# A graph network on one core: the column of dst on ScalarE's queue, and rows of the count matrix at one phase in SBUF

## The chip, the core and the metric

The kernel runs on one core of one Trainium2 chip. The metric is the device time of one execution in microseconds; the time given is the median of several runs. The core has five engines that run side by side, each with its own queue of instructions in program order: TensorE (PE in the profile; its weight loads are listed apart as PEld), VectorE (DVE), ScalarE (ACT), GpSimd (POOL) and SyncE (SP), which here issues DMAs. ScalarE and GpSimd issue some DMAs too. Each partition of SBUF, the memory on the chip, is addressed in bytes, and a tile takes the same byte range in all 128 partitions.

## The reference

A layer norm and a ReLU over 2500 nodes of 256 features, three graph convolutions with the mean over 80000 edges (sorted by dst), a last linear layer over all four states, and the input added at the end:

```python
h = jnp.maximum(_layernorm(x, axis=-1), 0.0)
def _edge_conv(x, src, dst, W, b):
    xi = x[dst]
    xj = x[src]
    m = jnp.concatenate([xi, xj - xi], axis=-1) @ W + b
    s = jax.ops.segment_sum(m, dst, num_segments=N)
    cnt = jax.ops.segment_sum(jnp.ones((dst.shape[0],), m.dtype), dst, num_segments=N)
    return s / jnp.maximum(cnt, 1.0)[:, None]
...
xs = [h]
for W, b in ((W0, b0), (W1, b1), (W2, b2)):
    h = jax.nn.relu(_edge_conv(h, src, dst, W, b))
    xs.append(h)
return x + jnp.concatenate(xs, axis=-1) @ Wf + bf
```

## The kernel before

The kernel never gathers rows of features. It builds the matrix A whose entry (s, d) is the number of edges from node s to node d, and multiplies with it. The nodes d are cut into 417 windows of 6, and the windows into five groups: four of 84 windows (504 columns) and one of 81 (486 columns). The nodes s are cut into 20 tiles of 128. A group's part of A is one SBUF tile `a` of 128 partitions by 20 rows by G = 504 f32 columns (`new_a`, L733), and there are two such buffers, one in each of two pools, used in turn. With 504 columns a row is 2016 bytes long, and the next row follows at once.

**Start (before about 66 us).** The inputs are loaded in a fixed order: `dst` whole on ScalarE's queue (L396), then x in four chunks on SP and ScalarE (L400 to L410). `next_i` (L407 and L408) is a column of dst: for 127 partitions one number each, 4 bytes, 2500 bytes apart in memory, so that each partition knows the first edge of the next partition. From it VectorE makes `after`, `behind` and `pick` (`find_first`, `find_rows`); TensorE multiplies `pick` with `dst` (`pick_half`) and so finds where each window's edges begin; GpSimd then fetches the edges by an indirect DMA. Beside this, VectorE takes the statistics of x (`st`), ScalarE or GpSimd normalizes (`N`), TensorE turns the tiles round (`T`) and multiplies by the weights (`Z` with wb, `F` with wf). All of this stands in one order written out by hand as a string of short names (L849 to L858), which `perform` plays; objects ending in `o` (`SPo`, `ACTo`, `DVEo`) keep program order on their queue, while plain `SP`, `PE`, `DVE` leave it to a scheduler. Before the first pick TensorE runs 22 matmuls on zeros (`warm22`).

**Layer 0 (about 66 to 214 us).** For each group, VectorE compares edge keys with counters (`compare`, tiles one_m and one_n), TensorE multiplies the two 0/1 tiles (`counts`), and ScalarE copies the counts into `a` (`take_counts`). When a group's `a` is ready it is stored to DRAM (`finish`, L788), to be loaded again in layers 1 and 2 (`load_a`, L794). While a group is being built, TensorE multiplies with the group before it (`layer`).

**Layers 1 and 2 (about 214 to 498 us).** For each layer, `nodes_split` (L692) multiplies the states by wb and splits the product into two parts, zh and zl, as float32r; then for each group `layer` (L802) runs, for each of the 20 rows of `a`, four matmuls with that row as the moving operand (L817), then eight in plain f32 with the weights wt (L821), and `final` (L715) adds the last linear layer's share. The order of the groups is such that the two that are still in SBUF come first.

**Small constants.** `brow` holds the three biases, in one partition only (the one of the padding node, `PAD`); `ident` is an identity matrix for turning tiles. Both lie in the pool `const`, which lives through the whole kernel. The pool `pre` (`pp`) lives only through the start, and its space is given to the second buffer of A later.

Of the kernel before, what the change touches and what calls it, by code (L numbers as in the profile page):

```python
# [8 lines left out]
F32 = mybir.dt.float32  # L9
I32 = mybir.dt.int32  # L10
AF = mybir.ActivationFunctionType
OP = mybir.AluOpType
# [4 lines left out]
def general(ctx: ExitStack, tc: tile.TileContext, x, src, dst, Ws, bs, Wf, bf, out):  # L17
# [12 lines left out]
    EB = J * P  # L30
    G = 512
    NG = NP // G
    TG = G // P
    KL = 5
    CELLS = NP * NP
    BIG = 4096.0
    assert E == NCH * P and NCH == NB * J and NP % G == 0 and NT % KL == 0 and EB < BIG
    assert CELLS + EB < 2 ** 24
# [84 lines left out]
    def count_block(b):  # L123
        row = ps_big.tile([P, 2, G], F32, name="big").rearrange("p a n -> p (a n)")
        for j in range(J):
            c = b * J + j
            nc.tensor.transpose(row[:, j * P:(j + 1) * P], key[:, c:c + 1].to_broadcast([P, P]), ident)
        found = bwork.tile([P, J], F32, name="found")
        for j in range(J):
            c = b * J + j  # L130
            junk = bwork.tile([P, EB], F32, name="junk", bufs=1)
            nc.vector.scalar_tensor_tensor(junk, row[:, :EB], key[:, c:c + 1], weight[:, j, :],
                                           op0=OP.is_equal, op1=OP.mult, accum_out=found[:, j:j + 1])
        cell = bwork.tile([P, J], F32, name="cell")
        nc.vector.scalar_tensor_tensor(cell, found, BIG, past[:, b, :], op0=OP.is_lt, op1=OP.mult)
        cell_i = bwork.tile([P, J], I32, name="cell_i")
        nc.vector.tensor_add(cell_i, cell, spare)
        adds = []
        for j in range(J):
            d = nc.gpsimd.indirect_dma_start(  # L140
                out=at[:, :], out_offset=bass.IndirectOffsetOnAxis(ap=cell_i[:, j:j + 1], axis=0),
                in_=found[:, j:j + 1], in_offset=None, compute_op=OP.add)
            for o in adds:
                tc.declare_no_dep(d.ins, o.ins, reason="distinct cells within a block")
            behind(d)
            adds.append(d)
        latest[:] = adds
# [51 lines left out]
    def group(l, g):  # L199
        hl, hn = h[l % 2], h[(l + 1) % 2]  # L200
        pa = ps_big.tile([P, 2, G], F32, name="big")
        if l == 0:
# [39 lines left out]
    for l in range(L):  # L242
        for g in range(NG):
            group(l, g)
# [21 lines left out]
F32R = mybir.dt.float32r  # L266
# [20 lines left out]
def run(it):  # L287
    for _ in it:
        pass
# [16 lines left out]
def chain(*its):  # L306
    for it in its:
        yield from it
# [3 lines left out]
def by_windows(ctx: ExitStack, tc: tile.TileContext, x, src, dst, Ws, bs, Wf, bf, out, missing):  # L312
    nc = tc.nc
    PE, DVE, ACT, POOL, SP = nc.tensor, nc.vector, nc.scalar, nc.gpsimd, nc.sync
    PEo, DVEo, POOLo, ACTo, SPo = (InOrder(tc, e) for e in (PE, DVE, POOL, ACT, SP))
    P = 128
    N, D = x.shape
    E = src.shape[0]
    NT = (N + P - 1) // P
    NP = NT * P  # L320
    LAST = N - (NT - 1) * P
    L = len(Ws)
# [13 lines left out]
    while sum(GWS) < NW:  # L336
        GWS.append(min(84, NW - sum(GWS)))
    G = max(GWS) * W
    NG = len(GWS)
    Q = NT // 2  # L340
    assert NT == 2 * Q
    PAD = 96
# [7 lines left out]
    const = ctx.enter_context(tc.tile_pool(name="const", bufs=1))  # L350
# [9 lines left out]
    def bank():  # L360
        return ps[-1].tile([P, 512], F32, name="bank")
# [8 lines left out]
    away = const.tile([P, WG, CAP], BF16, name="away")  # L370
    cnt = const.tile([P, NP], BF16, name="cnt")
    share = const.tile([P, NT], F32, name="share")
    brow = const.tile([P, L, D], F32, name="brow")
    bf_sb = const.tile([P, D], F32, name="bf_sb")
    ident = const.tile([P, P], F32, name="ident")
    ones = const.tile([P, 1], F32, name="ones")
    ones_b = const.tile([1, 1], BF16, name="ones_b")
    ident_b = const.tile([P, P], BF16, name="ident_b")
# [4 lines left out]
    nc_ = const.tile([P, W + 2], F32, name="nc_")  # L383
    deg_b = const.tile([P, WG, W], BF16, name="deg_b")
    lim = const.tile([P, WG], F32, name="lim")
    a_dram = [dram.tile([P, NT, G], F32, name=f"a_dram{g}") for g in range(NG)]

    apools = [ctx.enter_context(tc.tile_pool(name="apool0", bufs=1))]
    pre = ctx.enter_context(ExitStack())
    pp = pre.enter_context(tc.tile_pool(name="pre", bufs=1))  # L390
    pw = pre.enter_context(tc.tile_pool(name="prework", bufs=2))


    dst_rows = dst.rearrange("(p c) -> p c", p=P)
# [5 lines left out]
    def load_x(queue, a, b):  # L400
        queue.dma_start(acc[:, a:min(b, NT - 1), :], xr[:, a:min(b, NT - 1), :])
        if b == NT:
            queue.dma_start(acc[:LAST, NT - 1, :], x[(NT - 1) * P:N, :])

    chunks = [(0, 2), (2, 6), (6, 12), (12, NT)]
    load_x(SPo, *chunks[0])
    next_i = pp.tile([P, 1], I32, name="next_i")  # L407
    SPo.dma_start(next_i[:P - 1], dst_rows[1:P, 0:1])  # L408
    load_x(SPo, *chunks[1])
    load_x(ACTo, *chunks[2])  # L410
    ws = [None] * L
# [2 lines left out]
    def load_wb(l, queue=SP):  # L414
        ws[l] = wpool.tile([P, DC, D], F32, name="wt"), wpool.tile([P, DC, D], F32, name="wb", bufs=1)
        queue.dma_start(ws[l][1], Ws[l][D:2 * D, :].rearrange("(c p) d -> p c d", p=P))

    def load_wt(l, queue=SP):
        queue.dma_start(ws[l][0], Ws[l][0:D, :].rearrange("(c p) d -> p c d", p=P))
# [19 lines left out]
    POOL.memset(brow, 0.0)  # L439
    nc_i = pp.tile([P, W + 2], I32, name="nc_i")  # L440
    POOL.iota(nc_i, pattern=[[-1, W + 2]], base=1, channel_multiplier=0)
    for l in range(L):
        SP.dma_start(brow[PAD:PAD + 1, l, :], bs[l].rearrange("(o d) -> o d", o=1))
    DVE.memset(ones, 1.0)
    DVE.memset(ones_b, 1.0)
    DVE.memset(cnt[:, NV:], 0.0)
# [199 lines left out]
    turned, pz = {}, {}  # L646
# [45 lines left out]
    def nodes_split(l, t):  # L692
        pz = bank()
        for c in range(DC):
            PE.matmul(pz[:, :D], hT[:, c, t * P:(t + 1) * P], ws[l][1][:, c, :],  # L695
                      start=(c == 0), stop=(c == DC - 1))
        sc = share[:, t:t + 1]
        if t == NT - 1:
            zf = hot.tile([P, D], F32, name="zf")
            DVE.scalar_tensor_tensor(zf, pz[:, :D], sc, brow[:, l, :], op0=OP.mult, op1=OP.add)  # L700
            ACT.copy(zh[:, t, :], zf)
            DVE.tensor_sub(zl[:, t, :], zf, zh[:, t, :].bitcast(F32))
        else:
            ACT.activation(zh[:, t, :], pz[:, :D], AF.Copy, scale=sc)  # L704
            DVE.scalar_tensor_tensor(zl[:, t, :], pz[:, :D], sc, zh[:, t, :].bitcast(F32),  # L705
                                     op0=OP.mult, op1=OP.subtract)

    def add_x(t):
        n = P if t < NT - 1 else LAST
        xb = hot.tile([P, D], F32, name="zf")  # L710
        POOL.dma_start(xb[:n], x[t * P:t * P + n, :])
        POOL.tensor_add(xb[:n], xb[:n], bf_sb[:n])
        POOL.tensor_add(acc[:n, t, :], acc[:n, t, :], xb[:n])
# [15 lines left out]
    def touched(g):  # L729
        c0, n = group_of(g)  # L730
        return [t for t in range(NT) if (t + 1) * P > c0 and t * P < c0 + n]

    def new_a(g):  # L733
        return apools[g % 2].tile([P, NT, G], F32R, name="a")

    windows = [(g, s, min(BW, GWS[g] - s)) for g in range(NG) for s in range(0, GWS[g], BW)]
    ones_of = {}
# [47 lines left out]
    def finish(g, a):  # L785
        c0, n = group_of(g)
        POOLo.tensor_copy(a[PAD:PAD + 1, NT - 1, :n], cnt[PAD:PAD + 1, c0:c0 + n])
        SP.dma_start(a_dram[g][:, :, :n], a[:, :, :n].bitcast(F32))  # L788
        yield
# [43 lines left out]
    a = new_a(0)  # L833
# [39 lines left out]
    def later_loads():  # L873
        load_wb(1, SPo)
        load_wt(1, SPo)
        load_wf(1, SPo)
        SPo.dma_start(bf_sb, bass.AP(tensor=bf.tensor, offset=bf.offset, ap=[[0, P], [1, D]]))
        yield
# [5 lines left out]
    extra = chain(degrees(0), finish(0, a), later_loads(), degrees(1))  # L884
    for g in range(NG):
        at = {}
        own = LATE
        if g + 1 < NG:
            a1 = new_a(g + 1)
# [20 lines left out]
        if g + 1 < NG:  # L910
            run(finish(g + 1, a1))
            held, a = a, a1
# [3 lines left out]
    for l in range(1, L):  # L916
        groups = list(range(NG))
        if l % 2:
            groups.reverse()

        last = touched(groups[0])
        for t in [t for t in range(NT) if t not in last] + last:
            nodes_split(l, t)
        if l + 1 < L:
            load_wb(l + 1)
            load_wt(l + 1)
        finished = set()
        for j, g in enumerate(groups):
            for t in touched(g):
                if t not in finished:  # L930
                    finished.add(t)
                    final(l, t)
                    if l == 1:
                        add_x(t)
            if j == NG - 1:
                load_wf(l + 1)
            run(layer(l, g, tiles[g], LATE))
            if j == 1 and l + 1 < L:
                DVEo.tensor_sub(ws[l + 1][0], ws[l + 1][0], ws[l + 1][1])
            if j + 2 < NG:  # L940
                del tiles[g]
                tiles[groups[j + 2]] = load_a(groups[j + 2])
# [41 lines left out]
```

## Time and profile before

| What | Value |
|---|---|
| median of 3 runs | 521.25 us (520.58 to 522.91) |
| the profiled execution | 522.35 us |
| its span in the profile | 520.4 us |
| mean granted clock of TensorE | 0.997 |
| matmuls on A in layers 1 and 2 (L817) | 800 |
| matmuls on A in layer 0 (line of a helper, L280) | 400 |
| store of one 504-column group of A, issue to landing | 15.4 us (5040 KB) |
| load of one | 15.8 us |
| the same for the 486-column group | 17.1 us and 15.7 us (4860 KB) |

The profile is one execution, told in several views. The page's first part gives each engine's busy time. The chain of waits follows the work that ended last back from the end: what stands in it sets the time, what does not is covered. A group row names the line, the engine, the operation, the tiles as out<-in, the shape and the count, then the busy time and the mean of one, then the engine's idle time just before. Most instructions of the start have the line of a helper, L280, so that they are told apart by their tiles. Matmuls overlap in the pipeline, so their real pace is the distance from start to start.

### The profile page before, as it was taken

Reading aid. Unit: us, or ns where it says so; the run is one execution under the profiler, and the core shown is the slowest. Engines: PE = TensorE matmul, PEld = TensorE weight load, DVE = VectorE, ACT = ScalarE, POOL = GpSimd, SP = SyncE. Lnnn points to the kernel's source line nnn. Section 1 sums busy time; section 2 is a strip of 40 time slices with the busy share of each in tenths; the row PEclk is TensorE's granted clock in tenths of the full one; section 3 lists DMA queues with packets and bytes.
Section 4 is the critical chain, followed back from the end, with each engine's and each line's share of the span. In section 5 each row is a group of like instructions: output and inputs, shape, how many; then the busy total and the mean of one; then the engine's idle time right before and its main releaser. Section 6 shows DMA issues by size and latency. Waiting matters only on the chain.

```text
span 520.4 us, 6987 instructions
## 1 busy us (share of the span) xinstructions
PE 512.0 (98%) x2864; PEld 406.8 (78%) x2864; DVE 213.8 (41%) x455; ACT 138.2 (27%) x307; POOL 69.8 (13%) x102
## 2 busy tenths in 40 slices
PE   7999999999999999999999999999999999999996
PEld 3888878677777778788787878787887878787875
DVE  6899989888797950251101010102501010101033
ACT  5787567553633330340000000003400000000000
POOL 2591000000000000008133323200000000000000
PEclk9999999999999999999999999999999999999999
DMA  9110008840905319001556464100006363630023
GB/s 277 38 51 1 1 2 342 323 203 1 398 1 246 153 34 359 23 20 52 201 232 244 204 247 192 31 1 1 1 0 243 155 248 150 238 145 20 1 82 122
DMA packets 16351, 68.74 MB, mean 132 GB/s; under 512 B 1328, under 2 KB 14152, under 8 KB 15158
## 3 DMA queue, kind: packets, MB, share of 16 engines
q1 hardware_dynamic: 14038, 63.49, 31.2%
q0 software_dynamic: 1344, 3.61, 2.3%
q10 hardware_dynamic: 928, 1.11, 0.7%
q8 instruction: 24, 0.39, 0.3%
q14 instruction: 17, 0.14, 0.1%
HBM read 40.03 MB, written 28.18 MB: 131 GB/s over the span
## 4 chain that ended last, share of the span: by engine, by line
PE 96%; DVE 1%; DMA 1%; issue 0%; ACT 0%; SPq 0%
PE pa L817 35%; PE pa L280 21%; PE bank L718 10%; PE bank L280 9%; PE bank L695 7%; PE pa L821 6%; PE pz L280 6%; DMA next_i<-in_dst_dram 1%; PE turned L280 1%; DVE one_m L280 0%; DVE one_n L280 0%; ACT junk L280 0%; DVE pick L280 0%; DVE zl L280 0%; ACT hT L280 0%
## 5 line engine op out<-in xcount | busy, mean ns | idle before, releaser
L817 PE MATMUL pa<-a,zh 128*128 128x504 f32 (+1 forms) x400 | 157.6, 394 | 0.0
L817 PE MATMUL pa<-a,zl 128*128 128x504 f32 (+1 forms) x400 | 155.5, 389 | 0.0
L720 DVE SCALAR_TENSOR_TENSOR acc<-bank,share,acc 128x256 f32<-128x256 f32 x60 | 29.0, 484 | 214.8 <-PE bank L718 214.8
L817 PEld LDWEIGHTS pa<-a,zh 128*128 128x128 f32 x400 | 75.3, 188 | 15.6
L817 PEld LDWEIGHTS pa<-a,zl 128*128 128x128 f32 x400 | 75.2, 188 | 15.3
L280 PE MATMUL pa<-a,zh 128*128 128x504 f32 (+1 forms) x200 | 85.1, 426 | 0.0
L280 DVE TENSOR_TENSOR one_m<-iota_m,key_m 128x1024 bf16<-128x1024 bf16 (+1 forms) x105 | 71.9, 685 | 15.7 <-PE bank L280 15.4
L280 PE MATMUL pa<-a,zl 128*128 128x504 f32 (+1 forms) x200 | 77.8, 389 | 0.0
L824 ACT ACTIVATE hT<-pa 128x1008 f32<-128x1008 f32 (+1 forms) x10 | 10.0, 1005 | 240.2 <-PE pa L821 240.2
L280 ACT CAST a<-bank 128x480 fp32r<-128x480 f32 (+1 forms) x105 | 54.5, 561 | 66.7 <-PE bank L280 63.9
L280 DVE TENSOR_TENSOR one_n<-iota_n,key_n 128x960 bf16<-128x960 bf16 (+1 forms) x105 | 68.6, 653 | 0.0
L280 PEld LDWEIGHTS <-one_m 128*128 128x128 bf16 x834 | 45.6, 98 | 14.2 <-DVE one_m L280 7.5
L280 PE MATMUL bank<-one_n,one_m 128*128 128x120 bf16 x834 | 54.1, 217 | 0.3 <-DVE one_n L280 0.2
L718 PE MATMUL bank<-wf,hT 128*128 128x256 f32 x240 | 53.6, 379 | 0.0
L718 PEld LDWEIGHTS bank<-wf,hT 128*128 128x128 f32 x240 | 45.6, 190 | 9.9 <-issue 4.1
L280 PEld LDWEIGHTS pa<-a,zh 128*128 128x128 f32 x200 | 37.8, 189 | 9.1 <-issue 2.3
L280 PEld LDWEIGHTS pa<-a,zl 128*128 128x128 f32 x200 | 37.7, 189 | 8.2 <-issue 2.3
L705 DVE SCALAR_TENSOR_TENSOR zl<-bank,share,zh 128x256 fp32r<-128x256 f32 x38 | 18.4, 484 | 56.0 <-ACT zh L704 56.0
L821 PE MATMUL pa<-hT,wt 128*128 128x504 f32 (+1 forms) x80 | 35.2, 583 | 0.0
L695 PE MATMUL bank<-wb,hT 128*128 128x256 f32 x160 | 34.9, 379 | 0.0
L695 PEld LDWEIGHTS bank<-wb,hT 128*128 128x128 f32 x160 | 30.4, 190 | 4.9 <-issue 0.9
L821 PEld LDWEIGHTS pa<-hT,wt 128*128 128x128 f32 x80 | 15.2, 189 | 14.5 <-issue 13.8
(110 smaller groups left out, 339.2 us busy)
## 6 DMA issues: line engine op xcount, KB each, us to landing
a<-a_dram SPq DMA_DIRECT2D x5, 5040.0 KB, 15.8
a_dram<-a SPq DMA_DIRECT2D x4, 5040.0 KB, 15.4
a_dram<-a SPq DMA_DIRECT2D x1, 4860.0 KB, 17.1
a<-a_dram SPq DMA_DIRECT2D x1, 4860.0 KB, 15.7
zf<-in_x_dram POOLq DMA_DIRECT2D x19, 128.0 KB, 2.3
out_dram<-acc SPq DMA_DIRECT2D x19, 128.0 KB, 1.7
wf<-in_L_gnn_Wf_dram SPq DMA_DIRECT2D x4, 256.0 KB
acc<-in_x_dram SPq DMA_DIRECT2D x1, 896.0 KB, 8.4
```

The costliest lines, as they stand in the source:

```text
L280: return self.tc.keep_in_program_order(call(*args, **kwargs))
L695: PE.matmul(pz[:, :D], hT[:, c, t * P:(t + 1) * P], ws[l][1][:, c, :], start=(c == 0), stop=(c == DC - 1))
L705: DVE.scalar_tensor_tensor(zl[:, t, :], pz[:, :D], sc, zh[:, t, :].bitcast(F32), op0=OP.mult, op1=OP.subtract)
L718: PE.matmul(po[:, :D], hT[:, c, t * P:(t + 1) * P], wfs[l][:, c, :], start=(c == 0), stop=(c == DC - 1))
L720: DVE.scalar_tensor_tensor(acc[:, t, :], po[:, :D], share[:, t:t + 1], acc[:, t, :], op0=OP.mult, op1=OP.add)
L817: PE.matmul(pa[:, o, :n], z[:, i, o * P:(o + 1) * P], a[:, i, :n], start=(i == 0 and z is zh), stop=(z is zl and last[o] == (kind, i, o)))
L821: PE.matmul(pa[:, o, :n], ws[l][0][:, c, o * P:(o + 1) * P], hT[:, c, c0:c0 + n], start=False, stop=(last[o] == (kind, i, o)))
L824: ACT.activation(hT[:, :, c0:c0 + n], pa[:, :, :n], AF.Relu)
```

## The change

The column `next_i` is issued on ScalarE's queue, right behind `dst`, and ahead of SP's x chunks in the program. The row length of the tile `a` becomes GS = 512 elements (2048 bytes), of which the first 504 or 486 are used. To make room, `brow` keeps two biases instead of three (the third is loaded into the first's place ahead of layer 2), and `ident` goes from `const` to `pre`. A tile of 24 elements named `between` (96 bytes, never used) is put behind the constants; with it everything that is allocated after `const` begins at 64 modulo 128 bytes. In DRAM the rows of A stay 504 elements apart, so that a store or load of A moves one row at a time.

```diff
+    GS = 512
...
-    brow = const.tile([P, L, D], F32, name="brow")
+    brow = const.tile([P, 2, D], F32, name="brow")
...
-    ident = const.tile([P, P], F32, name="ident")
...
+    const.tile([P, 24], F32, name="between")
...
+    ident = pp.tile([P, P], F32, name="ident")
...
     chunks = [(0, 2), (2, 6), (6, 12), (12, NT)]
+    next_i = pp.tile([P, 1], I32, name="next_i")
+    ACTo.dma_start(next_i[:P - 1], dst_rows[1:P, 0:1])
     load_x(SPo, *chunks[0])
-    next_i = pp.tile([P, 1], I32, name="next_i")
-    SPo.dma_start(next_i[:P - 1], dst_rows[1:P, 0:1])
     load_x(SPo, *chunks[1])
     load_x(ACTo, *chunks[2])
...
-    for l in range(L):
-        SP.dma_start(brow[PAD:PAD + 1, l, :], bs[l].rearrange("(o d) -> o d", o=1))
+    def load_b(l, queue=SP):
+        queue.dma_start(brow[PAD:PAD + 1, l % 2, :], bs[l].rearrange("(o d) -> o d", o=1))
+
+    load_b(0)
+    load_b(1)
...
-            DVE.scalar_tensor_tensor(zf, pz[:, :D], sc, brow[:, l, :], op0=OP.mult, op1=OP.add)
+            DVE.scalar_tensor_tensor(zf, pz[:, :D], sc, brow[:, l % 2, :], op0=OP.mult, op1=OP.add)
...
-        return apools[g % 2].tile([P, NT, G], F32R, name="a")
+        return apools[g % 2].tile([P, NT, GS], F32R, name="a")
...
         if l + 1 < L:
+            load_b(l + 1)
             load_wb(l + 1)
             load_wt(l + 1)
```

## The prediction

> **What bounds the kernel now.** I read the busy line of the page first, then the chain that ended last, then the matmul groups with their shapes kept apart, and at last the first 17 us of the chain and the DMA landings.
>
> ```profile
> PE 512.0 (98%) x2864; PEld 406.8 (78%) x2864; DVE 213.8 (41%) x455; ACT 138.2 (27%) x307; POOL 69.8 (13%) x102
> ...
> PE 96%; DVE 1%; DMA 1%; issue 0%; ACT 0%; SPq 0%
> ...
> L817 PE MATMUL pa<-a,zh 128*128 128x504 f32 x320 | 126.5, 395 | 0.0
> L817 PE MATMUL pa<-a,zl 128*128 128x504 f32 x320 | 124.9, 390 | 0.0
> ...
> 285.18 18.28 PE pa L817 x80
> 303.46 3.38 PE pa L821 x8
> ```
>
> TensorE is busy 98% and is 96% of the chain: what counts is time per matmul, and the holes at the start. The "mean ns of one" of the group rows overlaps its neighbours; the chain gives the true pace: 80 matmuls of 504 columns in 18.28 us, 228.5 ns each. [...]
>
> [...] The built program puts the two A buffers at bytes 148320 and 188640, which is 96 and 224 modulo 256; rows are 2016 B apart, so each begins 32 B lower modulo 256 than the one before. Start to start in the trace, the four matmuls of one row (zh, zl, zh, zl) together, in ns, for the eight 504-column stages of layers 1 and 2, the first two rows and the last left out:
>
> ```
> row begins at (mod 256)    0    32    64    96   128   160   192   224
> four matmuls             917   917   902   918   913   920   910   917
> single ones at 192: 226, 229.5, 229, 226      at 64: 224, 224, 229.5, 224      at 160: 228, 234, 232.5, 225
> ```
>
> The same row number differs by 8 ns between the two buffers, and exactly as this table says, so it is the address, not the place in the stage. The mean is 914.
>
> Now the start:
>
> ```profile
> 1.25 6.42 DMA next_i<-in_dst_dram
> ...
> 7.70 0.15 DVE after L280
> ...
> 8.55 0.76 DVE pick L280
> ...
> 9.45 0.39 PE bank L280
> ...
> 11.66 3.62 PE pz L280 x8
> ...
> 7.70 0.15 DVE L280 CAST after<-next_i 127x1 f32<-127x1 int32 x1 [1.62 <-DMA next_i<-in_dst_dram]
> ...
> 8.45:11.86 3.41, 1.98 (x9) 1.32 (x10) 3.14 (x16) 2.79 (x10) 0.00 (x0) 1.00 1.11 336
> 11.86:15.28 3.42, 3.42 (x9) 2.71 (x9) 3.24 (x17) 1.93 (x7) 2.15 (x2) 0.50 0.51 147
> ```
>
> VectorE stands 1.62 us for the column, and TensorE, whose warm-up ends at about 8.0, waits for pick until 9.45. The last two rows are stages: their columns are busy PE, PEld, DVE, ACT, POOL, then the granted clock: after a thinly used 3.4 us the clock is half for the next 3.4, which costs some 1.7 us of TensorE's work.
>
> [...]the semaphore of next_i steps twice, at 1.72 and 7.67, where a 128-row load shows its engines one by one. [...]of the column's 4-byte packets some 84 run from 3.9 to 4.54, and the other 43 come one per 50 ns from 5.08 to 7.43, in turn with the 1 KB packets (47 ns) of ScalarE's x chunk.[...]
>
> **The change part by part.** *Rows of A.* Now 2048 B apart and the buffers at 146880 and 187840, both 192 modulo 256: every row of every stage begins in the phase that took 910 instead of the mean 914. There are 3 layers of 4 groups of 504 columns and 20 rows, 240 rows at 4 ns: 1.0 us less. For the 60 rows of 486 columns the trace has 881 at 192 against a mean of 882: nothing. What no run shows is a row that follows one of its own phase. Bounds from single matmuls: 224 each would be (228.5 - 224) x 1200 = 5.4 us less; 229.5 each 1.2 us more; 234.5, the highest seen (at 160), 7.2 us more. I take 910, the row as measured: the two cheapest of eight phases are the two that are 64 modulo 128.
>
> *Other matmul operands* (wt, wb, wf, one_m, one_n) move from 224 to 64 modulo 256 with the padding. Row L695 runs at 17.27/80 = 216 ns for 256 f32 columns[...]; nothing is taken, either way up to 0.5 us.
>
> *DMAs of A.* The full-width groups become 2560 pieces of 2016 B instead of 128 of 40320 B. The 486-column group already goes so: its store took 17.1 us against 15.4, its load 15.7 against 15.8. A full one would be 17.1 x 504/486 = 17.7. Loads are issued a stage (25 us) before their use at the least: hidden. Of the stores the first is tightest: issued at 80.84, it would land at 98.6, and the first write of group 2 into that buffer is at 99.89 (trace of ScalarE). Cover 1.3 us; beyond it, each us would stop ScalarE's evictions and then TensorE. Cost nothing. Behind it on SP stand the four loads of later_loads, wanted at 214 and later.
>
> *The column.* It goes from SP, between the first two x chunks, to ScalarE behind dst. On its one engine it begins when dst is through, 3.9, as before. It still has 127 pieces on one engine, and now takes turns with SP's chunks instead of ScalarE's chunk; 84 quickly and 43 at 50 ns end at 7.4 again. Bounds: alone it ends at about 5.2, before VectorE asks (6.08), and all 1.62 us go; in turns from the first, 127 x 57 ns from 3.9 ends at 11.1. I take no change in the landing. SP's issue of x rows 2 to 5, 2.43 us long behind the column now, should be short, and its landing (9.44; VectorE waits 0.17 for it) earlier: 0.2 us less. In exchange ScalarE's x chunk, its table load and the dst cast (4.28) stand behind the column: if ScalarE's issue takes those 2.4 us, the cast ends at about 6.2, where TensorE wants it at 9.4; the square root then comes at 6.2 and not 5.95, still ahead of the column. The chunk (tiles 6 to 11) then begins near 5.8 and shares with SP's until some 11.5, and the statistics of tiles 8 and 9, at 10.35 now, would be up to 1.2 us late. That delay is covered: VectorE idles 1.74 us at 17.82 for ScalarE.
>
> *Biases.* brow has two rows; the third bias is loaded into the first when with_b has read it (35.1). It stays ahead of A's first store in SP's order, so SP waits until 35, and has nothing to issue before 80.84: nothing. GpSimd's clearing of brow is a third shorter (0.80 us), beside nothing that waits. ident moves to the pool freed after the start; its readers end before that pool's space is reused for A. Nothing.
>
> Sum: 1.0 + 0.2 = 1.2 us less. The profiled execution took 522.35 (span 520.4 and 1.95 around it), 1.1 over the median of the three runs; it becomes 521.15, and the median 521.25 becomes 520.0.
>
> **The rivals.** *The rows lock into a cheap rhythm.* For: 224 three times of four at 64 modulo 256, and equal starts might make it lasting. Against: at 192 the two inner matmuls are 229. At 224 each: 521.25 - 5.4 - 0.2 = 515.6.
>
> *The column comes before it is asked for.* For: the first 84 pieces took 0.64 us; against: 43 in turns, on an engine that SP's chunks keep busy. TensorE could begin at 8.0, and the half clock might go as well, but the first F0 product needs wf, landed at 14.55, where it starts at 15.76 now: the gain stops at 1.2. 521.25 - 1.0 - 1.2 = 519.0.
>
> *The rows lock into a dear one* (the slower side). Place: all 1200 matmuls on A. For: equal phases within a row show 229.5 and 229 at 192; at 160 even 234. Against: 192 is below the mean as a whole. It makes the kernel slower from 228.5 ns on, by 0.5% from 230.7 on; at 234.5 it gives 528.3, at 231.5 524.7.
>
> *The column comes later*, in turns from its first piece: landing 11.1 + 0.2, 3.6 us later, and most of it on the path: 521.25 - 1.0 + 3.6 = 523.9.
>
> **How the numbers follow.** Chances: forecast 0.42, cheap rhythm 0.22, early column 0.14, dear rhythm 0.13, late column 0.09. Half a per cent (2.6 us) is what a measurement here can tell from no change: below 518.6 or above 523.9. Faster takes 0.20 of the cheap rhythm, 0.05 of the early column and 0.08 of the forecast's tail: 0.33. Slower takes 0.11 of the dear rhythm and 0.04 of the late column: 0.15. The rest, 0.52, is no change. The range runs from 516.0, which leaves out the strongest locking, to 524.0, which takes in the late column; alone, the forecast's own range is 518.5 to 522.
>
> **What would show it.** In the changed profile: the 80 matmuls of a 504-column stage in 18.2 us (18.28 now), rows alike from the second on; 17.9 would be the cheap rhythm, over 18.5 the dear one. The column's landing near 7.6 and VectorE's wait still about 1.6; a landing below 6.1 or above 9 refutes that step. SP's issue of x rows 2 to 5 below 1 us. Stores of A near 17.7 us, and no idle ScalarE near 99.9. The forecast is wrong if the stages on A move by more than 0.3 us each, or if another stage than these and the start changes.

## The result: 0.26% slower, and the profile after

The changed kernel takes 523.01 us (median of 22 executions, 522.30 to 523.88); the kernel before, run beside it, 521.45 (22 executions, 520.43 to 522.91). The ratio is 1.0026, with a 95% interval of 1.0017 to 1.0035: 1.4 us slower by the ratio and 1.6 by the medians, where the forecast had 1.2 us faster. It is under half a per cent, but the interval lies wholly above one. The execution profiled took 523.40 us, its span 521.6 against 520.4.

The page's busy line and shares of the chain, for the changed kernel:

```profile
PE 511.9 (98%) x2864; PEld 406.9 (78%) x2864; DVE 213.9 (41%) x455; ACT 138.2 (26%) x307; POOL 69.9 (13%) x102
...
PE 90%; DMA 3%; DVE 2%; POOL 2%; issue 1%; ACT 0%; ACTq 0%; DVEq 0%
```

TensorE's work is as long as before, but it has gone from 96% to 90% of the chain, and DMA and GpSimd stand in it. Where, the chain of waits of the changed kernel shows in order of time (start, length, what):

```profile
1.76 12.00 DMA acc<-in_x_dram
...
27.63 3.84 POOL acc L280 x2
34.02 2.10 POOL acc L280 x2
37.57 3.34 DMA es<-in_src_dram,start_i
...
287.21 18.15 PE pa L824 x80
```

Two things are to be read here. A 504-column stage (L824 is L817 of before) takes 18.15 us where it took 18.28. And the chain's first long piece is no longer the column (1.25 to 7.67) but ScalarE's x chunk, tiles 6 to 11 (1.76 to 13.76). VectorE's timeline of the changed kernel (start, busy, what, and in brackets the idle time before it and what ended it):

```profile
7.48 0.15 DVE L280 CAST after<-next_i 127x1 f32<-127x1 int32 x1 [1.38 <-DMA next_i<-in_dst_dram]
...
9.00 0.75 DVE L280 BATCH_NORM_STATS2 st<-acc 128x6 f32<-128x256 f32 x2
...
13.78 0.75 DVE L280 BATCH_NORM_STATS2 st<-acc 128x6 f32<-128x256 f32 x2 [3.82 <-DMA acc<-in_x_dram]
...
19.33 0.18 DVE L280 RECIPROCAL rs<-rs 128x4 f32<-128x4 f32 x1
```

The lines of the kernel before for the last two of these:

```profile
10.35 0.72 DVE L280 BATCH_NORM_STATS2 st<-acc 128x6 f32<-128x256 f32 x2
...
17.82 0.18 DVE L280 RECIPROCAL rs<-rs 128x4 f32<-128x4 f32 x1 [1.74 <-ACT rs L280]
```

The column comes 0.2 us sooner than before. The next statistics of SP's chunk start 0.46 us sooner. But then VectorE stands 3.82 us for ScalarE's chunk; in the kernel before it went straight on, at 10.35. ScalarE's timelines tell why, first of the kernel before, then of the changed one (ACTq is its sequencer issuing a DMA):

```profile
0.74 0.43 ACTq L280 DMA_DIRECT2D dst_i<-in_dst_dram  x1
1.20 0.45 ACTq L280 DMA_DIRECT2D acc<-in_x_dram  x1
```

```profile
1.19 0.53 ACTq L280 DMA_DIRECT2D next_i<-in_dst_dram  x1
1.76 2.59 ACTq L280 DMA_DIRECT2D acc<-in_x_dram  x1
```

The chunk's issue was through at 1.65 and is now through at 4.35. That is more than a shift of 2.7 us: meanwhile SP, whose queue is now clear, has issued its second chunk (1.26), wb (1.75) and its fourth chunk (2.30). In the trace's packets ScalarE's chunk begins at 7.97 instead of 3.78, just when wb has landed (7.96), and then moves side by side with SP's loads (755 of its packets and 760 of theirs from 8.2 to 13.0) until it lands at 13.76 instead of 7.95.

From there GpSimd carries the delay on. Its timeline before:

```profile
12.15 1.18 POOL L280 DMA_INDIRECT ed<-in_dst_dram,start_i  x1 [8.65 <-DVE off L280]
...
18.31 3.71 POOL L280 TENSOR_SCALAR acc<-acc,rs,off 128x256 f32<-128x256 f32 x6 [3.71 <-DVE off L280]
23.49 0.97 POOL L280 DMA_INDIRECT ed<-in_dst_dram,start_i  x1 [1.47 <-DVE start_i L280]
...
25.76 3.31 POOL L280 TENSOR_SCALAR acc<-acc,rs,off 128x256 f32<-128x256 f32 x2
...
33.88 0.97 POOL L280 DMA_INDIRECT ed<-in_dst_dram,start_i  x1 [0.16 <-issue]
```

and after:

```profile
15.61 1.18 POOL L280 DMA_INDIRECT ed<-in_dst_dram,start_i  x1 [12.33 <-DVE off L280]
...
19.82 3.70 POOL L280 TENSOR_SCALAR acc<-acc,rs,off 128x256 f32<-128x256 f32 x6 [1.75 <-DVE off L280]
25.36 0.97 POOL L280 DMA_INDIRECT ed<-in_dst_dram,start_i  x1 [1.84 <-DVE start_i L280]
...
27.63 3.84 POOL L280 TENSOR_SCALAR acc<-acc,rs,off 128x256 f32<-128x256 f32 x2
...
36.29 0.97 POOL L280 DMA_INDIRECT ed<-in_dst_dram,start_i  x1 [0.16 <-issue]
```

Subtract line from line: the first fetch of edges is 3.46 us late, because start_i stands behind the late statistics in VectorE's order. The slack ahead of the normalizing at 18.31 takes this down to 1.51. Then it grows again, for two reasons. To 1.87 by way of TensorE, whose products of pick and dst start_i needs: ahead of these, its first eight products with wf fall into a stretch at half clock (16.83 to 20.24, shown under "The clock" at the end) and take 3.39 us instead of 1.89. First the kernel before, then the changed one:

```profile
15.76 1.89 PE L280 MATMUL pz<-wf,hT 128*128 128x256 f32 x8
```

```profile
17.21 3.39 PE L280 MATMUL pz<-wf,hT 128*128 128x256 f32 x8
```

And to 2.41 because two normalizations on GpSimd take 3.84 us instead of 3.31; why, the trace does not say. From about 25 to 43 us none of GpSimd's idle times is over 0.31 us, so that no slack is left. VectorE gets the last fetched edges at 41.00 instead of 38.59, the same 2.41 late. The faster stages on A then take back some 0.3 us in layer 0 and 1.0 in layers 1 and 2 (eight stages at 0.13). 2.4 less 1.3 is 1.1; the spans differ by 1.2. How much of the 2.41 is this one execution's own, `column_only` below tells.

### The profile page after: what moved, and what is told of

Same layout as the page of the kernel before. It is cut to its first block, busy times and chain, and to the rows that moved or that the text cites. A ratio compares the mean times of both kernels' runs of the same rounds, so it can differ in the third digit from the quotient of the medians.

```text
span 521.6 us, 6987 instructions
## 1 busy us (share of the span) xinstructions
PE 511.9 (98%) x2864; PEld 406.9 (78%) x2864; DVE 213.9 (41%) x455; ACT 138.2 (26%) x307; POOL 69.9 (13%) x102
## 2 busy tenths in 40 slices
DMA packets 38239, 68.74 MB, mean 132 GB/s; under 512 B 1328, under 2 KB 37192, under 8 KB 38198
## 4 chain that ended last, share of the span: by engine, by line
PE 90%; DMA 3%; DVE 2%; POOL 2%; issue 1%; ACT 0%; ACTq 0%; DVEq 0%
PE pa L824 35%; PE pa L280 21%; PE bank L725 10%; PE bank L280 8%; PE bank L702 7%; PE pa L828 6%; PE pz L280 3%; DMA acc<-in_x_dram 2%; POOL acc L280 1%; DMA es<-in_src_dram,start_i 1%; DVE one_m L280 1%; POOL ed L280 1%; DVE one_n L280 0%; POOL es L280 0%; DVE zl L280 0%
## 5 line engine op out<-in xcount | busy, mean ns | idle before, releaser
L824 PE MATMUL pa<-a,zh 128*128 128x504 f32 (+1 forms) x400 | 156.8, 392 | 0.0
L824 PE MATMUL pa<-a,zl 128*128 128x504 f32 (+1 forms) x400 | 155.0, 387 | 0.0
L824 PEld LDWEIGHTS pa<-a,zh 128*128 128x128 f32 x400 | 75.2, 188 | 15.0
L824 PEld LDWEIGHTS pa<-a,zl 128*128 128x128 f32 x400 | 75.2, 188 | 15.0
L280 DVE TENSOR_TENSOR one_m<-iota_m,key_m 128x1024 bf16<-128x1024 bf16 (+1 forms) x105 | 72.3, 689 | 15.4 <-PE bank L280 15.2
## 6 DMA issues: line engine op xcount, KB each, us to landing
a<-a_dram SPq DMA_DIRECT2D x5, 5040.0 KB, 17.4
a_dram<-a SPq DMA_DIRECT2D x4, 5040.0 KB, 17.2
```

Source lines behind the costliest of these rows:

```text
L280: return self.tc.keep_in_program_order(call(*args, **kwargs))
L824: PE.matmul(pa[:, o, :n], z[:, i, o * P:(o + 1) * P], a[:, i, :n], start=(i == 0 and z is zh), stop=(z is zl and last[o] == (kind, i, o)))
```

## The experiments

The theory: the rows give a gain, and the start more than takes it back, because ScalarE's chunk comes late. Its rivals: that the new rows give nothing, that the column on ScalarE is dear in itself, or that TensorE's half-clock stretch, which not every execution has, makes the difference. Within the theory two causes of the late chunk were open: that ScalarE's sequencer stands behind the column, or that the chunk is issued after more of SP's loads. "Before" is below always the median of the kernel before, run beside the variant.

**The two halves of the change alone.** `rows_only` puts the column back on SP:

```diff
-    next_i = pp.tile([P, 1], I32, name="next_i")
-    ACTo.dma_start(next_i[:P - 1], dst_rows[1:P, 0:1])
     load_x(SPo, *chunks[0])
+    next_i = pp.tile([P, 1], I32, name="next_i")
+    SPo.dma_start(next_i[:P - 1], dst_rows[1:P, 0:1])
     load_x(SPo, *chunks[1])
```

> The changed kernel with the column back on SP, between the first two x chunks. Theory (the column's place costs the time, the rows of A win): the x chunk on ScalarE lands near 8.0 us again, VectorE's 3.8 us wait for it is gone, TensorE's first product with wf starts near 15.8 instead of 17.2, and the 504-column stages stay at 18.15 us; together 519.5 to 520.2 us, 1.3 to 1.9 us under before. Rival (the 2016-byte pieces of A's stores and loads, or the moved constants, cost it): the time stays near 523 although the start is as before.

`column_only` is the kernel before with nothing but the column moved:

```diff
-    load_x(SPo, *chunks[0])
     next_i = pp.tile([P, 1], I32, name="next_i")
-    SPo.dma_start(next_i[:P - 1], dst_rows[1:P, 0:1])
+    ACTo.dma_start(next_i[:P - 1], dst_rows[1:P, 0:1])
+    load_x(SPo, *chunks[0])
```

> The kernel before with only the column moved to ScalarE's queue behind dst. Theory: slower than before by what the start lost in the changed kernel, 2 to 3 us, so 523.5 to 524.6 us; the ScalarE chunk lands after 13 us; A's stages stay at 18.28 us. Rival (rows and padding cost it): 521.5, as before.

Before: 521.04. `rows_only`: 519.61 us, ratio 0.9975 (0.9964 to 0.9986). `column_only`: 524.09 us, ratio 1.0050 (1.0031 to 1.0069). The product of the two ratios is 1.0025, that of the whole change 1.0026: the halves add up, and have opposite signs. VectorE's timeline of `column_only` has the same new wait:

```profile
7.14 0.15 DVE L280 CAST after<-next_i 127x1 f32<-127x1 int32 x1 [1.03 <-DMA next_i<-in_dst_dram]
13.62 0.75 DVE L280 BATCH_NORM_STATS2 st<-acc 128x6 f32<-128x256 f32 x2 [3.99 <-DMA acc<-in_x_dram]
```

So the column came sooner (7.12; 7.67 in the kernel before), the chunk later, and the time went with the chunk. Its trace also gives the price of the late chunk at an equal clock, since its half-clock stretch is at 11.26, close to the 11.86 of the kernel before:

```profile
24.70 0.98 POOL L280 DMA_INDIRECT ed<-in_dst_dram,start_i  x1 [1.47 <-DVE start_i L280]
...
35.11 0.98 POOL L280 DMA_INDIRECT ed<-in_dst_dram,start_i  x1 [0.16 <-issue]
```

The fetches of edges are 1.21 and 1.23 us late, where the changed kernel's were 1.87 and 2.41, and layer 0's first matmul on A is 1.31 us late (65.77; 64.46 before), where the changed kernel's was 2.41 (66.87). So about half of the 2.41 comes with the late chunk at an equal clock; the rest is where the stretch fell in that one execution, and its two slower normalizations. The spans of `column_only` and before differ by 1.4 us (521.8 and 520.4); that the medians differ by more has to do with the clock too, and is taken up at the end. `rows_only` has no wait for the chunk, which landed at 8.15, and its 504-column stages take the 18.15 us of the changed kernel.

**Is it the sequencer that stands, or the place in the order of issue?** `split_act` leaves the column on ScalarE, but as two loads of 112 and 15 partitions. The first load's semaphore steps one by one, from 4.33 to 5.01, where that of the whole column steps twice (at 1.81 and 7.46 in the changed kernel); by this the first seems spread over the DMA engines and the whole column on one. If it is the column that holds the sequencer, the issue behind it should be short:

```diff
-    ACTo.dma_start(next_i[:P - 1], dst_rows[1:P, 0:1])
+    for p in ((0, 112), (112, P - 1)):
+        ACTo.dma_start(next_i[p[0]:p[1]], dst_rows[p[0] + 1:p[1] + 1, 0:1])
```

> The changed kernel with the column on ScalarE's queue as two loads, 112 partitions and 15. Theory[...]: ScalarE's issue of its x chunk falls from 2.59 us to about 0.5, the column lands before VectorE asks for it at about 6.1, the chunk lands near 8 to 10, and TensorE's picks begin right after the warm-up; 518.3 to 519.8 us. Rival (ScalarE's queue is slow behind SP's however the column is cut, since SP's chunks are ahead): issue short, but the chunk still lands after 12 us and the time stays near 522.

521.48 us, ratio 0.9995 (0.9982 to 1.0007), over the range expected; what was named there as the rival came. The column landed at 5.01 and 6.35, and the chunk's issue took 0.42 us instead of 2.59. VectorE still waits for the chunk:

```profile
6.45 0.15 DVE L280 CAST after<-next_i 127x1 f32<-127x1 int32 x1 [0.26 <-DMA next_i<-in_dst_dram]
...
12.44 0.75 DVE L280 BATCH_NORM_STATS2 st<-acc 128x6 f32<-128x256 f32 x2 [3.51 <-DMA acc<-in_x_dram]
```

The chunk's first packet is at 6.54, about when most of wb's semaphore steps come (6.49 to 6.79), and it lands at 12.42. Of the 5.81 us by which the changed kernel's chunk is late, 4.47 remain with a sequencer that does not stand; the standing is worth the other 1.34. The chunk's new place is the larger cause. That place has two sides, which no run separates: the column is ahead of the chunk in its own queue, and SP's second chunk and wb are issued ahead of it on the other. The kernel before speaks for the second side: there SP's second chunk, behind the whole column on SP, had its first packet at 5.86, 1.8 us after its issue was through and while the column was still under way; ScalarE's chunk needed 3.6 us in the changed kernel and 3.7 in `split_act`. A column ahead thus doesn't explain the whole wait. In time, `split_act` is 0.3% faster than the changed kernel by the ratios, of which the column's own earlier landing may have a part.

**The chunk away from behind the column.** `chunk_sp` keeps the column on ScalarE as changed and issues the chunk on SP, behind SP's second:

```diff
     load_x(SPo, *chunks[1])
-    load_x(ACTo, *chunks[2])
+    load_x(SPo, *chunks[2])
```

> The changed kernel (whole column on ScalarE behind dst) with the third x chunk, tiles 6 to 11, taken from ScalarE's queue to SP's, right behind the second chunk. Theory (the harm is that this chunk is issued after SP's three loads and so served late; the column itself does no harm where it is): the chunk lands near 9, VectorE's 3.8 us wait for it is gone, ScalarE's table load and dst cast are early again, and the time is that of rows_only or less, 518.8 to 519.8 us. Rival (a column on ScalarE's queue slows the start in itself, for instance by taking turns with SP's loads): 521 us or more.

Before: 521.54. `chunk_sp`: 519.33 us, ratio 0.9966 (0.9956 to 0.9977). The chunk landed at 9.37, ahead of its use; the column at 7.19. The column on ScalarE is thus not dear in itself.

`act_last` keeps the chunk on ScalarE and ahead of the column, which is issued as the third:

```diff
-    ACTo.dma_start(next_i[:P - 1], dst_rows[1:P, 0:1])
     load_x(SPo, *chunks[0])
...
     load_x(ACTo, *chunks[2])
+    ACTo.dma_start(next_i[:P - 1], dst_rows[1:P, 0:1])
```

> The changed kernel with ScalarE's two loads swapped: dst, the third x chunk, then the column. Theory (order of issue over both queues decides who is served first): the chunk is issued near 1.2 us and lands near 7 to 8 as before; the column lands after it, 7.5 to 9, so VectorE waits 1.5 to 3 us for it and the rest follows; 519.5 to 521 us. Rival (ScalarE's queue is served after SP's whatever the order): the chunk still lands after 12 us, 523 us.

528.45 us, ratio 1.0137 (1.0116 to 1.0158): over 7 us above the range expected. The chunk did as the theory says: its first packet was at 3.82 and it landed at 8.16. The column did not, as VectorE's timeline shows:

```profile
14.90 0.15 DVE L280 CAST after<-next_i 127x1 f32<-127x1 int32 x1 [9.01 <-DMA next_i<-in_dst_dram]
```

Behind the chunk, its 127 pieces began at about 7.0, when SP's 1 KB packets moved too, and came four or five per 0.25 us until 14.43. In the changed kernel some 90 of the 4-byte pieces passed between 4.0 and 4.75. This is the late column among the prediction's rivals, which a place behind dst avoids.

**Both waits gone on SP.** `split_sp` is the changed kernel with the column back on SP in its old place, but in two loads:

```diff
-    ACTo.dma_start(next_i[:P - 1], dst_rows[1:P, 0:1])
     load_x(SPo, *chunks[0])
+    for p in ((0, 112), (112, P - 1)):
+        SPo.dma_start(next_i[p[0]:p[1]], dst_rows[p[0] + 1:p[1] + 1, 0:1])
     load_x(SPo, *chunks[1])
```

> The changed kernel with the column back on SP between the first two x chunks, and as two loads, 112 partitions and 15. Theory: SP's issue of the second x chunk falls from 2.43 us to about 0.5, VectorE's wait for the column (1.6 us) goes, the gain stops at the landing of wf near 14.5; 518.5 to 519.8 us, up to 1.2 under rows_only. Rival (the start is bound by the loads as a whole): same as rows_only.

519.03 us beside a before of 521.04, ratio 0.9948 (0.9930 to 0.9966). The column landed at 6.05 and 6.95, SP's next issue took 0.43 us (2.47 in `rows_only`), and ScalarE's chunk, not moved, landed at 7.00.

The starts side by side, from the packets and landings in the traces (the medians were taken beside befores of 521.04, 521.45 and 521.54):

```
the third x chunk:  issue begins  through  first packet  landed   column landed   median us
before                  1.20        1.65       3.78       7.95        7.67          521.45
changed                 1.76        4.35       7.97      13.76        7.46          523.01
column_only             1.76        4.11       7.64      13.60        7.12          524.09
split_act               2.38        2.80       6.54      12.42        6.35          521.48
act_last                1.19        1.64       3.82       8.16       14.88          528.45
```

**The phase of the rows.** Four kernels, one execution each, are `rows_only` with another padding, which puts every row of A at 64, 96, 128 or 160 modulo 256 instead of 192. The rows stay 2048 bytes apart. The other operands behind the constants move along.

```diff
-    const.tile([P, 24], F32, name="between")
+    const.tile([P, 56], F32, name="between")
```

(56 elements for 64; no such tile for 96; 8 elements for 128; 16 for 160.)

> The rows-only kernel (column on SP) with the padding such that both buffers of A begin at 64 modulo 256 instead of 192. Theory (the phase modulo 256 decides as in the table of the kernel before): rows at about 902 ns, a 504-column stage at 18.05 us instead of 18.15. Rival (once all rows have one phase only the phase modulo 128 counts): 907 and 18.15 as at 192.

> The same without the padding tile, so that the buffers begin at 96 modulo 256. Theory (each phase keeps its time): rows at 917 ns, a stage at 18.35 us, no gain from the distance of 2048 bytes alone. Rival (the distance alone wins): 907 and 18.15.

> The same at 128 modulo 256. Theory (each phase keeps its time): rows at 913 ns, a stage at 18.27 us. Rival (the distance alone wins): 907 and 18.15.

> The same at 160 modulo 256, the dearest phase of the kernel before. Theory (each phase keeps its time): rows at 920 ns, a stage at 18.4 us. Rival (equal row phases settle into one rhythm whatever the phase is, so that the equal distance and not the phase wins): 907 and 18.15.

From the chains of waits, a 504-column stage of layers 1 and 2 each, in the order `phase064`, `phase096`, `phase128`, `phase160`:

```profile
284.48 18.16 PE pa L824 x80
```

```profile
283.49 18.31 PE pa L823 x80
```

```profile
283.20 18.39 PE pa L824 x80
```

```profile
285.36 18.14 PE pa L824 x80
```

And by rows, start to start in the traces, the four matmuls of one row together, in ns; the first line is the kernel before, where each row begins 32 bytes lower than the one before it, the second the kernels in which all rows begin alike:

```
row begins at (mod 256)       64     96    128    160    192
before, phases in turn       902    918    913    920    910
all rows at this phase       907    916    920    907    907
```

The whole times of these single executions (520.64, 520.84, 520.85 and 521.39, beside a before of 520.75) say little, since executions of one kernel differ by 2 us; the stages hardly differ. Even starts alone give nothing: at 96 and 128 the stage is longer than the 18.28 of before. The phase counts (18.14 us at 160, 18.39 at 128), but not by the table of before: 160, there the dearest, is as good as 192. So what a row cost in the old table was not its own phase's doing alone. The neighbour's phase is the likely rest, but the other operands moved too, and no run keeps them in place.

**Put together.** `split_sp_064` is `split_sp` with A at 64 modulo 256, where the 486-column row was cheaper as well (866.7 ns in one stage, 880 in the other, 884.5 at 192). `chunk_sp_split` has A at 64 too, the column on ScalarE in two loads and the third chunk on SP:

```diff
-    const.tile([P, 24], F32, name="between")
+    const.tile([P, 56], F32, name="between")
...
-    ACTo.dma_start(next_i[:P - 1], dst_rows[1:P, 0:1])
+    for p in ((0, 112), (112, P - 1)):
+        ACTo.dma_start(next_i[p[0]:p[1]], dst_rows[p[0] + 1:p[1] + 1, 0:1])
...
-    load_x(ACTo, *chunks[2])
+    load_x(SPo, *chunks[2])
```

> split_sp (column on SP in two loads) with the padding that puts A at 64 modulo 256. From the profiles: 504-column stages as at 192 (906.6 ns a row), 486-column stages 866.7 instead of 884.5 ns a row, 60 rows, 1.1 us less: 517.6 to 518.4 us. Rival (the other tiles that move by 128 bytes, the one-hot tiles and weights, cost as much): 519, as split_sp.

> The column on ScalarE behind dst in two loads (112 and 15 partitions), the third x chunk on SP behind the second, A at 64 modulo 256. Theory: the column lands near 5 to 6, before or about when VectorE asks for it at 6.1; picks begin right after the warm-up near 8.1; then wf bounds the start: 517 to 518.4 us, at or under split_sp_064. Rival (all loads together bound the start, so whoever is brought forward pushes another back): same as split_sp_064 or slower.

`split_sp_064`: 518.84 us, ratio 0.9951 (0.9934 to 0.9968) beside a before of 521.54. Its profiled span is 0.3 us under that of `split_sp`, not the 1.1 expected: one of the two 486-column stages of layers 1 and 2 has its gain (0.36 us), the other next to none. `chunk_sp_split`: 518.63 us, 0.2 above its range, ratio 0.9946 (0.9928 to 0.9964); the column landed at 5.03 and 6.39, the chunk at 9.01. The two and `split_sp` can't be told apart. Each is about 0.5% faster than the kernel before and, by the ratios, 0.8% faster than the changed one.

## Why the prediction was wrong

**The step that failed** is this one, in its words: the chunk "begins near 5.8 and shares with SP's until some 11.5, and the statistics of tiles 8 and 9, at 10.35 now, would be up to 1.2 us late. That delay is covered: VectorE idles 1.74 us at 17.82 for ScalarE". The chain of events was the right one, its two sizes were not. The chunk began at 7.97 and landed at 13.76, and the statistics were 3.43 us late. That ScalarE's issue would stand 2.4 us was seen (2.59 came). What was not priced is the wait behind it: the forecast let the chunk share the engines with SP's loads from 5.8 on, but in the changed kernel its first packet came 3.6 us after its issue was through, with SP's second chunk and wb ahead of it, and `split_act` shows that 4.47 us of the lateness stay when the issue is short. The cover was real and did its part: VectorE's idle 1.74 us at 17.82 have gone, and 3.43 us came out there as 1.5 (17.82 to 19.33 for the same instruction). But it was half of what was needed (3.43 - 1.74 leaves 1.7), so that something was left to pay where the sum put nothing: 1.3 us in `column_only`'s trace, where the half-clock stretch lies as in the kernel before. The cover was also looked for on one engine only: GpSimd, which fetches the edges behind the same statistics, has no slack after about 25 us (no idle time over 0.31 us) and hands a delay on, so that in the changed kernel's trace a half-clock stretch and slower normalizations made 2.41 of it. By the ratio, which counts executions with and without the stretch, `column_only` puts the whole edit at +0.5%, 2.6 us, against the 0.2 us less that the sum had.

**Rows of A.** Right in kind, too small: 0.13 us per stage of 504 columns, twelve of them, less 0.04 for each of three of 486, is 1.4 us by the stages, where 1.0 was taken. `rows_only` measures 0.25%, 1.3 us. The step took the row at 192 from the table of before; the phase runs show that this table can't be read row by row, so that the number came out near by luck of the phase chosen (at 128 the same reasoning would have erred in sign). The cheap and the dear rhythm didn't come: 226.7 ns per matmul was neither 224 nor 229.5.

**The column's landing.** Right: 7.46 for "7.4 again", and a wait of 1.38 us for "about 1.6". The early column came only with the split load, the late one only in `act_last`.

**SP's issue of x rows 2 to 5.** Right: the two first chunks are now issued in 0.97 us together, and the wait of 0.17 us for the second has gone. But that gain and the loss go together: what lets SP's loads go sooner puts them ahead of ScalarE's chunk.

**The stores and loads of A.** Right: 17.2 us for a store (17.7 predicted, 15.4 before), 17.4 for a load, over twice the packets in all (38239), and no wait from it. **Biases and ident**: no wait came from them, as said.

**The range** ended at 524.0 because of the late column, and so held 523.01 by luck, through another mechanism than the one it was drawn for. The slower outcome by a late chunk was not among the rivals.

## What to carry to other kernels

A small load put at the head of one engine's queue can cost that queue's next load its place, here against the other queue's loads and behind the small load itself: before moving it, list all loads by the time of their issue over both queues, as it will be after the move, and put a price on the wait of the one that falls behind (here 3.6 us from the end of its issue to its first packet, with 768 KB of SP's issued ahead of it). A delay is covered only if every engine that stands behind it has slack (here VectorE had 1.74 us, GpSimd after about 25 us at most 0.31 at a time); read the idle time of each of them up to the point where they meet, not of the first alone. The column of one number per partition was better issued as 112 and 15 partitions than as 127, on either queue: the next issue took 0.42 and 0.43 us instead of 2.59 and 2.47. And before two traces are subtracted, see in both where the half-clock stretch lies.

## What the runs showed of the hardware

**Order over two queues.** Between 4.35, when the issue of ScalarE's chunk was through, and 7.97 SP's loads moved 1250 packets of 1 KB and the chunk none; from 8.2 to 13.0 it was 755 of the chunk's and 760 of SP's. Behind the column in one load the next issue took 2.59 us on ScalarE (the changed kernel) and 2.43 on SP (the kernel before), behind the column in two loads 0.42 (`split_act`) and 0.43 (`split_sp`). Why the chunk's first packet came only at 7.97, when 15 of wb's 16 semaphore steps had come from 6.55 to 7.04, the runs leave open; it is 3.6 us after its issue was through, and 3.7 in `split_act`.

**float32r rows.** The pace of a matmul on A goes with where its row begins: 226.7 ns at 64, 160 or 192 modulo 256, 229 at 96, 230 at 128, for 504 columns in rows of 2048 bytes; the other operands moved along. The start is not all of it: with both buffers at 64, one 486-column stage took 866.7 ns a row and the other 880. What makes it so isn't known from these runs.

**The clock.** The half-clock stretch that the profile of before has at 11.86 comes later in the changed kernel (windows of its profile: stretch, length, then busy PE, PEld, DVE, ACT, POOL, granted clock, DMA share, GB/s):

```profile
12.00:16.83 4.83, 2.36 (x11) 1.40 (x10) 2.94 (x17) 1.92 (x6) 1.18 (x1) 1.00 0.23 71
16.83:20.24 3.41, 3.41 (x10) 2.78 (x11) 3.33 (x17) 2.26 (x10) 1.40 (x2) 0.50 0.26 79
```

In both traces it is 3.41 us long, at a granted clock of 0.50. Other executions of the same kernel are without it, as far as the recorded mean clocks tell. Of 43 executions of the kernel before, run beside `column_only`, 27 had a mean granted clock of at least 0.998 and a median of 520.75 us, 16 had less and 522.45: 1.7 us, half of such a stretch. The traces agree on the price: of the kernels that issue their loads at the start in the order of before, `phase064` and `phase160` have the stretch and begin layer 0's matmuls on A at 64.44 and 65.02 us (before: 64.46), `rows_only`, `phase096` and `phase128` have none and begin at 62.78 to 62.98. Of the changed kernel's 22 executions, 20 had a mean clock under 0.998; of `column_only`'s six, all; of `split_sp`'s six, none.

So `column_only`'s 2.6 us have two parts. Its median is 1.6 us above before's executions with the lower clock, in fair agreement with the 1.3 and 1.4 of the two traces; the rest comes from being set beside a before in which 27 of 43 executions had the higher clock. Whether the hole left by the late chunk brings the stretch on is open. In the changed kernel's trace the stretch comes right behind the hole (TensorE was busy for 0.94 us of the 3.41 before it), but in `column_only`'s it begins at 11.26, as in the kernel before, ahead of the hole. Nor is the stretch the whole price: the two executions of the changed kernel with the higher clock took 522.30 and 522.40 us, 1.6 above before's 520.75, though its rows save 1.3. Only one execution of each kernel was traced; the others are told apart by their mean clocks alone.
